# Summing a state-space scan over its states by accumulating transposes instead of identity matmuls

## The chip, the cores and the metric

The kernel runs on one core of one Trainium2 chip. A core has five engines that work side by side, each through its own list of instructions in order: TensorE (PE, with its weight loads shown as PEld), VectorE (DVE), ScalarE (ACT), GpSimd (POOL) and SyncE (SP, which here issues the transfers). They wait for one another through semaphores. The metric is the device time of one execution in microseconds (us), the median of three runs.

## The reference

The reference chains four layers over 8 images of 192 channels and 64 x 64 positions. Layers 0 and 2 each hold a selective state-space scan in four directions (rows, columns, and both reversed), and these two scans per image are what the change is about. For each direction, per channel c and state n (16 states):

```python
xs = jnp.stack([x_hw, x_wh, x_hw[..., ::-1], x_wh[..., ::-1]], axis=1)
x_dbl = jnp.einsum('kdc,bkcl->bkdl', x_proj_w, xs)
dts, Bs, Cs = (x_dbl[:, :, :R], x_dbl[:, :, R:R + N], x_dbl[:, :, R + N:])
dt = jax.nn.softplus(jnp.einsum('kcr,bkrl->bkcl', dt_proj_w, dts) + dt_proj_b[None, :, :, None])
A = -jnp.exp(A_log)
...
def step(h, inp):
    dt_t, B_t, C_t, x_t = inp
    h = h * jnp.exp(dt_t[..., None] * A[None]) + (dt_t * x_t)[..., None] * B_t[:, :, None, :]
    return (h, jnp.einsum('bkcn,bkn->bkc', h, C_t))
_, ys = jax.lax.scan(step, h0, (dt_l, Bs_l, Cs_l, xs_l))
ys = jnp.moveaxis(ys, 0, 3) + Dp[None, :, :, None] * xs
```

So the state h is a first-order recurrence along 4096 positions, and the output at a position is the sum over the 16 states of h times C. The four directions are added up at the end. All numbers are float32.

## The kernel before, in words

The kernel runs the images one after the other. For each there are two calls of `scan_layer`, and between them the rest of the layers, which the change leaves alone. There are 16 scans in all.

**Units.** Channels are on the 128 partitions; the four scan directions with 192 channels fill three such blocks, v = 0, 1, 2 (v = 2 holds the 64 remaining channels of two directions), and a forward pass (d = 0) and a backward pass (d = 1). A pass goes over the positions in 8 chunks of Q = 512. One unit is (d, chunk, v): 2 x 8 x 3 = 48 units in a scan. A group m is the three units of one chunk. Within a unit the 512 positions are four blocks of 128 (NB = 4, SB = 128), and the tile `da` is laid out as 128 x [4 blocks, 16 states, 128 positions].

**A unit's work.** It is done in eight steps j = 0..7; two steps make one block, one for each half of the states.
- `fill` (L288, PE) makes the driving term u for a step in PSUM, by 16 or 32 small matmuls of 32 rows. Tile `u` has two buffers.
- `scan` (L304, L306, L309, DVE) runs the recurrence over 8 states x 128 positions in place in `da`.
- `times_c` (L326, POOL) multiplies a finished block by C, which `load_c` (L263, L266) has brought in as a broadcast of 1 MB; then L329 (POOL) adds the top three or four states' planes onto lower ones, so that 12 or 13 planes of 16 are left to sum (NP = 12).
- `add_up` (L344, L349, PE) adds the planes over the states: matmuls of the identity with 512 positions of one state, accumulating in the PSUM tile `py`. The table SUM says how many come in each step. The sums of unit k-1 run during unit k, from step 2 on.
- `finish` (L372 or L376, DVE) takes the sum out of PSUM two units later, at step 2. In the forward pass it adds the skip term and stores the result to the DRAM tensor `yp`; in the backward pass it adds what `load_y` has fetched of `yp` and stores to `ys`.

**Preparation of the next unit.** `steps_a` (PE, L212 or L214), `steps_b` (ACT softplus, L218) and `steps_c` (POOL, L222) make the time steps and their product with the input. `turn` transposes that product at step 2 on PE (L230) and ACT copies it out (L232, then four pieces L235). `decay` (L245, ACT) makes the 16 exponentials of the next unit's `da` at steps 2 to 6, and `cut` (L254, L255) and `keep` (L316) hand over the ends of blocks and chunks at step 7. For the next group, `project_a` and `project_b` (L147, L154, L157) stand at steps 0 and 1 of v = 0, `diagonals_a` (L187) at step 5 of v = 1 and step 1 of v = 2, and `diagonals_b` (DVE, L197) at steps 6 and 7 of both.

**What sets the order.** The whole scan stands under a hand-written order: each engine works through its instructions as the loop over k and j lists them, and waits where data or a buffer are missing. In one step the loop lists scan, (step 7) cut and keep, times_c and load_c, steps_c, fill of the next step, finish, load_y, turn, projections and diagonals, add_up, decay.

**PSUM** is full: `da0` one bank, `u` four, `misc` two, `py` one. `misc` is shared by turn, the projections, steps_a and diagonals_a. At step 4 of v = 0, two `misc` buffers are taken by steps_a for the next group; they are read by the softplus at step 1 of v = 1. `da` has three buffers, `ct` three.

Of the kernel before, what the change touches and what calls it, by code (L numbers as in the profile page):

```python
# [40 lines left out]
def tile_net(ctx: ExitStack, tc: tile.TileContext, a: dict, out: bass.AP):  # L41
# [23 lines left out]
    yp = [dram.tile([P, T], F32, name=f"yp{i}") for i in range(3)]  # L65
# [33 lines left out]
    def scan_layer():  # L99
# [5 lines left out]
        with (  # L105
# [11 lines left out]


            NP = 12
# [6 lines left out]
            dts, dtx, dtt, das, cts, us, py, yo = {}, {}, {}, {}, {}, {}, {}, {}  # L126
# [5 lines left out]
            def misc():  # L132
                return sp.tile([P, Q], F32, tag="misc", name="misc", bufs=2)
# [86 lines left out]
            def steps_c(k):  # L220
                dtx[k] = sw.tile([P, Q], F32, tag="dtx", name="dtx")
                nc.gpsimd.tensor_tensor(dtx[k], dts[k], vt[k // 3][:, units[k][3], :], ALU.mult)  # L222
# [95 lines left out]
            def times_c(k, g):  # L318
                h = das[k][:, NB - 1 - g if units[k][0] else g]
                if k == nu - 1 and g == NB - 1:  # L320

                    ct = cts.pop((k, g))
                    for eng, n in ((nc.gpsimd, slice(0, 8)), (nc.vector, slice(8, NS))):
                        eng.tensor_tensor(h[:, n], h[:, n], ct[:, n], ALU.mult)
                    return
                nc.gpsimd.tensor_tensor(h, h, cts.pop((k, g)), ALU.mult)  # L326
                n = NS - NP if g < 2 else NS - NP - 1
                to = h[:, NP - n : NP]
                nc.gpsimd.tensor_tensor(to, to, h[:, NS - n : NS], ALU.add)  # L329

            def load_y(k):
                d, i, c, v = units[k]
                yo[k] = sw.tile([P, Q], F32, tag="yo", name="yo")
                if d:
                    nc.sync.dma_start(out=yo[k], in_=yp[v][:, c * Q : (c + 1) * Q])

            to_add = []

            def add_up(count):

                for k, n in to_add[:count]:
                    if n == 0:
                        py[k] = sp.tile([P, Q], F32, tag="py", name="py")
                    nc.tensor.matmul(  # L344
                        py[k], ident, das[k][:, :, n, :], start=(n == 0), stop=(n == NP - 1)
                    )
                    if n == 8:
                        s = slice(0, NB // 2) if units[k][0] else slice(NB // 2, NB)
                        nc.tensor.matmul(  # L349
                            py[k][:, s.start * SB : s.stop * SB], ident, das[k][:, s, NP, :],  # L350
                            start=False, stop=False,
                        )
                del to_add[:count]

            def add_last(g0, g1):

                k = nu - 1
                if k not in py:
                    py[k] = misc()
                s = slice(NB - g1, NB - g0)  # L360
                ns = NS if g1 == NB else NP + (g0 == 2)
                for n in range(ns):
                    nc.tensor.matmul(  # L363
                        py[k][:, s.start * SB : s.stop * SB], ident, das[k][:, s, n, :],
                        start=(n == 0), stop=(n == ns - 1),
                    )

            def finish(k):
                d, i, c, v = units[k]
                p, y = py.pop(k), yo.pop(k)  # L370
                if d == 0:
                    nc.vector.scalar_tensor_tensor(  # L372
                        y, vt[k // 3][:, v, :], skip[:, v : v + 1], p, ALU.mult, ALU.add
                    )
                else:
                    nc.vector.tensor_tensor(y, y, p, ALU.add)  # L376
                nc.sync.dma_start(out=(ys if d else yp)[v][:, c * Q : (c + 1) * Q], in_=y)

            SUM = ((1, 0, 1, 2, 0, 2, 1, 2), (2, 2, 1, 1, 1, 2, 2, 2), (2, 1, 1, 2, 2, 2, 2, 2))
            DECAY = {2: (0, 3), 3: (3, 7), 4: (7, 9), 5: (9, 12), 6: (12, 16)}

            def has(k):
                return 0 <= k < nu
# [27 lines left out]
            for k in range(nu + 1):  # L413
                m, v = divmod(k, 3)
                ahead = 0 <= m + 1 < nm
                for j in range(8):
# [20 lines left out]
                    if j == 2:  # L437
                        if has(k - 2):
                            finish(k - 2)
                        if k == nu:  # L440
                            finish(k - 1)
                        if has(k - 1) and k < nu:
                            load_y(k - 1)
                        if has(k + 1):
                            turn(k + 1)
# [20 lines left out]
                    if (k, j) == (nu - 1, 3):  # L466
                        load_y(k)
                    if j == 2 and has(k - 1) and k < nu:
                        to_add += [(k - 1, n) for n in range(NP)]
                    add_up(SUM[v][j])  # L470
                    if (k, j) == (nu - 1, 7):
                        add_last(0, 2)
                    if (k, j) == (nu, 0):
                        add_up(NP)
                        add_last(2, 3)
                        add_last(3, 4)
# [880 lines left out]
```

## Time and profile before

| | |
|---|---|
| median of three runs | 25583.9 us (25560.59 to 25592.02) |
| span of the profiled execution | 25584.6 us |
| one scan, first to last recurrence (16 of them, the 4th as example) | 1154.9 us |
| DMA over the span | 4294 MB, mean 168 GB/s |
| ACT copy of 128 x 512 out of PSUM (L232), mean | 587 ns |
| exponentials (L245), mean of one | 699 ns, 12544 of them |
| PE matmuls of the sums (L344), mean of one | 627 ns, 18048 of them |
| PE matmuls of the turn (L230), mean of one | 317 ns, 3072 of them |

The profile page gives, for each engine, the time in which it was busy and its share of the span. PE's time is that of overlapping matmuls, so its share says how long something was in flight and not how near PE is to its limit; the start of one group and the start of the next say more. The groups list for each line of the kernel the number of instructions, the busy time, the mean of one, and the idle time before it with what ended it. The chain of waits is followed back from the last instruction. In answers by stretch of time, each engine has its busy time with the number of instructions in brackets, then come the granted TensorE clock as a share of full speed, the share of the DMA engines, and GB/s. In a timeline, a line is start, duration, engine, line, operation, tiles and the number of instructions merged.

### The profile page before, as it was taken

Reading aid. Unit: us, or ns where it says so; the run is one execution under the profiler, and the core shown is the slowest. Engines: PE = TensorE matmul, PEld = TensorE weight load, DVE = VectorE, ACT = ScalarE, POOL = GpSimd, SP = SyncE. Lnnn points to the kernel's source line nnn. Section 1 sums busy time; section 2 is a strip of 40 time slices with the busy share of each in tenths; the row PEclk is TensorE's granted clock in tenths of the full one; section 3 lists DMA queues with packets and bytes.
Section 4 is the critical chain, followed back from the end, with each engine's and each line's share of the span. In section 5 each row is a group of like instructions: output and inputs, shape, how many; then the busy total and the mean of one; then the engine's idle time right before and its main releaser. Section 6 shows DMA issues by size and latency. Waiting matters only on the chain.

```text
span 25584.6 us, 433060 instructions
## 1 busy us (share of the span) xinstructions
PE 23083.5 (90%) x174856; PEld 12129.3 (47%) x174856; DVE 20590.3 (80%) x21253; ACT 14175.8 (55%) x23120; POOL 19097.7 (75%) x7436
## 2 busy tenths in 40 slices
PE   9989889898898988989889898898988989899896
PEld 4535445353453534535345353553535535355353
DVE  7969789697896968969689696886968879688795
ACT  5646456464564645646456564555645556455563
POOL 7939589395893958939589395894958949589495
PEclk9989989899998999989999899998999989899898
DMA  5636556365563655636556365663655636566364
GB/s 168 207 116 203 145 173 207 117 202 146 174 206 115 204 146 171 206 117 204 141 177 204 120 202 138 180 202 119 204 134 182 202 120 204 131 185 204 118 204 117
DMA packets 1204805, 4293.98 MB, mean 168 GB/s; under 512 B 360224, under 2 KB 419456, under 8 KB 804480
## 3 DMA queue, kind: packets, MB, share of 16 engines
q1 hardware_dynamic: 1202816, 4266.25, 56.3%
q8 instruction: 1395, 22.86, 0.4%
q14 instruction: 594, 4.87, 0.1%
HBM read 3810.55 MB, written 450.72 MB: 167 GB/s over the span
## 4 chain that ended last, share of the span: by engine, by line
POOL 36%; PE 13%; DVE 5%; ACT 4%; issue 3%; DMA 2%; SPq 0%; POOLq 0%; DVEq 0%; ACTq 0%
POOL da L326 27%; POOL da L329 6%; PE py L344 3%; PE u L288 2%; POOL dtx L222 2%; DVE da L309 2%; PE pa L530 1%; ACT da L245 1%; PE pa L533 1%; DMA a<-t 1%; PE misc L363 1%; DVE pwc L986 0%; DMA t<-u 0%; PE paa L530 0%; PE pac L530 0%
## 5 line engine op out<-in xcount | busy, mean ns | idle before, releaser
L309 DVE TENSOR_TENSOR_SCAN da<-da,u 128x1024 f32<-128x1024 f32 x6144 | 14042.1, 2286 | 325.4 <-ACT da L255 37.0
L326 POOL TENSOR_TENSOR da<-da,ct 128x2048 f32<-128x2048 f32 x3056 | 13859.0, 4535 | 319.9 <-DVE tmp L304 297.3
L344 PE MATMUL py<-da,ident 128*128 128x512 f32 x18048 | 9304.0, 627 | 504.0 <-POOL da L326 407.0
L288 PEld LDWEIGHTS u<-dg,dtt 32*128 32x128 f32 x131072 | 5943.9, 163 | 4598.2 <-issue 4309.6
L245 ACT ACTIVATE da<-dt,neg_a 128x512 f32<-128x512 f32 (+1 forms) x12544 | 7662.1, 699 | 16.3
L288 PE MATMUL u<-dg,dtt 32*128 32x128 f32 x131072 | 7234.0, 283 | 120.7 <-DVE da L309 48.2
L344 PEld LDWEIGHTS py<-da,ident 128*128 128x128 f32 x18048 | 3043.1, 191 | 2998.5 <-issue 2134.8
L329 POOL TENSOR_TENSOR da<-da 128x512 f32<-128x512 f32 (+1 forms) x3056 | 3474.4, 1137 | 239.6
L222 POOL TENSOR_TENSOR dtx<-dt,vt 128x512 f32<-128x512 f32 x768 | 979.1, 1276 | 3310.1 <-ACT dt L218 2621.4
L232 ACT COPY dtt<-misc 128x512 f32<-128x512 f32 x768 | 450.4, 587 | 3343.3 <-PE misc L230 3343.3
L306 DVE TENSOR_TENSOR u<-u,tmp 128x8 f32<-128x8 f32 x5952 | 1009.9, 170 | 1081.2 <-PE u L288 860.0
L235 ACT COPY dtt<-misc 32x512 f32<-32x512 f32 x3008 | 1734.7, 577 | 45.3
L197 DVE TENSOR_TENSOR dg<-msk,misc 128x1024 f32<-128x1024 f32 x1024 | 1222.9, 1197 | 439.1 <-DMA vt<-vs 239.3
L161 ACT ACTIVATE xd<-misc,msk 128x512 f32<-128x512 f32 x256 | 175.7, 686 | 1790.7 <-PE misc L157 1790.7
L218 ACT ACTIVATE dt<-misc 128x512 f32<-128x512 f32 x768 | 430.8, 595 | 1101.7 <-PE misc L214 1096.7
L974 POOL TENSOR_TENSOR acc<-u,gate 128x486 f32<-128x486 f32 (+1 forms) x80 | 108.5, 1360 | 962.0 <-DVE u L989 688.8
L930 POOL MEMSET t<- 128x4356 f32 (+2 forms) x32 | 100.5, 3140 | 932.7 <-DVE t L904 914.6
L968 PE MATMUL pwc<-t,l3taps 128*128 128x486 f32 (+1 forms) x1280 | 590.7, 610 | 40.2 <-DVE t L989 20.1
L230 PE MATMUL misc<-ident,dtx 128*128 128x128 f32 x3072 | 592.7, 317 | 0.0
L187 PE MATMUL misc<-ident,xd 16*128 16x16 f32 x4096 | 565.5, 266 | 26.0 <-DVE dg L197 26.0
L986 DVE SCALAR_TENSOR_TENSOR pwc<-t,l3p,pwc 128x486 f32<-128x486 f32 (+1 forms) x640 | 467.0, 736 | 136.6 <-PE pwc L968 123.8
L187 PEld LDWEIGHTS misc<-ident,xd 16*128 16x128 f32 x4096 | 528.2, 210 | 92.7 <-issue 88.9
(291 smaller groups left out, 18289.2 us busy)
## 6 DMA issues: line engine op xcount, KB each, us to landing
ct<-cd SPq DMA_DIRECT2D x2048, 1024.0 KB
ct<-cd SPq DMA_DIRECT2D x2048, 512.0 KB
vt<-vs SPq DMA_DIRECT2D x768, 256.0 KB
yp<-yo SPq DMA_DIRECT2D x384, 256.0 KB
yo<-yp SPq DMA_DIRECT2D x384, 256.0 KB
ys<-yo SPq DMA_DIRECT2D x384, 256.0 KB
yt<-ys SPq DMA_DIRECT2D x96, 512.0 KB
t<-ys SPq DMA_DIRECT2D x96, 512.0 KB
```

The lines of the kernel that those rows point to most:

```text
L187: nc.tensor.transpose(pt[:, i * NS : (i + 1) * NS], xd[m][rows, cols], ident[rows, rows])
L197: nc.vector.tensor_tensor(dg[m, o][:, at], msk[:, 0:32].unsqueeze(1).unsqueeze(1).to_broadcast(shape), bts[m, o][:, at, r * 8 : r * 8 + 8] ...
L222: nc.gpsimd.tensor_tensor(dtx[k], dts[k], vt[k // 3][:, units[k][3], :], ALU.mult)
L230: nc.tensor.transpose(pt[:, i * P : (i + 1) * P], dtx[k][:, cols], ident)
L235: (nc.scalar.copy if k else nc.vector.tensor_copy)(dtt[k][q * 32 : (q + 1) * 32, 1], pt[r * 32 : (r + 1) * 32])
L245: nc.scalar.activation(das[k][:, s, n, :], dts[k].rearrange("p (s t) -> p s t", t=SB)[:, s], AF.Exp, scale=neg_a[:, v, d, n : n + 1],)
L288: nc.tensor.matmul(u[ch, r * 4 : r * 4 + 4, e::4], dtt[k][rows, r, e, ch], dg[k // 3, o][rows, r * 4 + e, n], start=True, stop=True,)
L306: nc.vector.tensor_tensor(head, head, tmps[k][:, n], ALU.add)
L309: nc.vector.tensor_tensor_scan(h, h, u.rearrange("p n t -> p (n t)")[:, way], 0.0, ALU.mult, ALU.add)
L326: nc.gpsimd.tensor_tensor(h, h, cts.pop((k, g)), ALU.mult)
L329: nc.gpsimd.tensor_tensor(to, to, h[:, NS - n : NS], ALU.add)
L344: nc.tensor.matmul(py[k], ident, das[k][:, :, n, :], start=(n == 0), stop=(n == NP - 1))
```

## The change

- `times_c` no longer adds planes together: L327 to L329 go.
- `add_up` no longer multiplies by the identity with the data as the moving operand. It takes one plane of 128 positions of one state as the stationary operand, in transpose mode, with the identity moving, and accumulates the 16 states of a block in PSUM. The result `py` is turned: positions on the partitions, channels along the free dimension. There are 16 transposes for a block, eight in a step, and a block's transposes begin two steps after its product with C is listed. So a unit's sums run from its own step 4 to step 3 of the next.
- `take` is new: at step 4 of the next unit ACT copies `py` to the tile `yt`. In the forward pass that is stored at once to `yp`, which now is positions by channels in DRAM.
- `load_y` fetches `yp` in that form at step 2, in the backward pass only, into one buffer instead of two.
- `turn_back` is new, backward pass only: at step 6 eight transposes on PE turn this pass's sums and the stored ones back and add them, in a `misc` buffer.
- `finish` now is in the backward pass only, at step 7: it adds the skip term and stores to `ys`.
- `dtx` has one buffer instead of two. The table SUM, the constant NP and the special end `add_last` go.

```diff
-                n = NS - NP if g < 2 else NS - NP - 1
-                to = h[:, NP - n : NP]
-                nc.gpsimd.tensor_tensor(to, to, h[:, NS - n : NS], ALU.add)
+            def positions(v, c):
+                return yp[v][c * Q : (c + 1) * Q].rearrange("(s t) c -> t s c", s=NB)
...
                 if d:
-                    nc.sync.dma_start(out=yo[k], in_=yp[v][:, c * Q : (c + 1) * Q])
+                    yo[k] = sw.tile([P, NB, P], F32, tag="yo", name="yo", bufs=1)
+                    nc.sync.dma_start(out=yo[k], in_=positions(v, c))
...
+            def add_up(block, part):
+                k, g = divmod(block, 4)
+                if g == 0 and part == 0:
+                    py[k] = sp.tile([P, NB, P], F32, tag="py", name="py")
+                s = NB - 1 - g if units[k][0] else g
+                for n in range(part * 8, part * 8 + 8):
                     nc.tensor.matmul(
-                        py[k], ident, das[k][:, :, n, :], start=(n == 0), stop=(n == NP - 1)
+                        py[k][:, s], das[k][:, s, n, :], ident, is_transpose=True,
+                        start=(n == 0), stop=(n == NS - 1),
                     )
...
+            def take(k):
+                d, i, c, v = units[k]
+                yt[k] = sw.tile([P, NB, P], F32, tag="yt", name="yt")
+                nc.scalar.copy(yt[k], py.pop(k))
+                if d == 0:
+                    nc.sync.dma_start(out=positions(v, c), in_=yt.pop(k))
+            def turn_back(k):
+                pb[k] = misc()
+                new, old = yt.pop(k), yo.pop(k)
+                for s in range(NB):
+                    for x in (new, old):
                         nc.tensor.matmul(
+                            pb[k][:, s * P : (s + 1) * P], x[:, s], ident, is_transpose=True,
+                            start=(x is new), stop=(x is old),
                         )
...
             def finish(k):
+                y = sw.tile([P, Q], F32, tag="y", name="y", bufs=1)
+                nc.vector.scalar_tensor_tensor(
+                    y, vt[k // 3][:, v, :], skip[:, v : v + 1], pb.pop(k), ALU.mult, ALU.add
+                )
+                nc.sync.dma_start(out=ys[v][:, c * Q : (c + 1) * Q], in_=y)
...
-                    add_up(SUM[v][j])
...
+                    if has(k - 1) and j == 4:
+                        take(k - 1)
+                    block = (8 * k + j - 4) // 2
+                    if 0 <= block < 4 * nu:
+                        add_up(block, j % 2)
+                    if has(k - 1) and units[k - 1][0]:
+                        if j == 6:
+                            turn_back(k - 1)
+                        if j == 7:
+                            finish(k - 1)
                     if has(k + 1) and j in DECAY:
                         decay(k + 1, *DECAY[j])
```

More of the change, by code (lines that the diff above doesn't have):

```diff
@@ L64, in tile_net @@
     ys = [dram.tile([P, T], F32, name=f"ys{i}") for i in range(3)]
-    yp = [dram.tile([P, T], F32, name=f"yp{i}") for i in range(3)]
+    yp = [dram.tile([T, P], F32, name=f"yp{i}") for i in range(3)]
     a_scr = dram.tile([192, T], F32, name="a_scr")
@@ L116, in scan_layer @@
             nck = T // Q
-            NP = 12
             units = [
@@ L125, in scan_layer @@
             vt, xd, cdr, dg = {}, {}, {}, {}
-            dts, dtx, dtt, das, cts, us, py, yo = {}, {}, {}, {}, {}, {}, {}, {}
+            dts, dtx, dtt, das, cts, us = {}, {}, {}, {}, {}, {}
+            py, yo, yt, pb = {}, {}, {}, {}
             def chunk_of(m):
@@ L220, in steps_c @@
             def steps_c(k):
-                dtx[k] = sw.tile([P, Q], F32, tag="dtx", name="dtx")
+                dtx[k] = sw.tile([P, Q], F32, tag="dtx", name="dtx", bufs=1)
                 nc.gpsimd.tensor_tensor(dtx[k], dts[k], vt[k // 3][:, units[k][3], :], ALU.mult)
@@ L326, in times_c @@
                 nc.gpsimd.tensor_tensor(h, h, cts.pop((k, g)), ALU.mult)
-                n = NS - NP if g < 2 else NS - NP - 1
-                to = h[:, NP - n : NP]
-                nc.gpsimd.tensor_tensor(to, to, h[:, NS - n : NS], ALU.add)
+            def positions(v, c):
+                return yp[v][c * Q : (c + 1) * Q].rearrange("(s t) c -> t s c", s=NB)
             def load_y(k):
                 d, i, c, v = units[k]
-                yo[k] = sw.tile([P, Q], F32, tag="yo", name="yo")
@@ L334, in load_y @@
                 if d:
-                    nc.sync.dma_start(out=yo[k], in_=yp[v][:, c * Q : (c + 1) * Q])
[L337 to L343, printed above, removed]
+                    yo[k] = sw.tile([P, NB, P], F32, tag="yo", name="yo", bufs=1)
[6 more added lines that the diff above has]
+                for n in range(part * 8, part * 8 + 8):
@@ L344, in add_up @@
                     nc.tensor.matmul(
-                        py[k], ident, das[k][:, :, n, :], start=(n == 0), stop=(n == NP - 1)
-                    )
-                    if n == 8:
-                        s = slice(0, NB // 2) if units[k][0] else slice(NB // 2, NB)
+                        py[k][:, s], das[k][:, s, n, :], ident, is_transpose=True,
+                        start=(n == 0), stop=(n == NS - 1),
+                    )
+            def take(k):
[4 more added lines that the diff above has]
+                    nc.sync.dma_start(out=positions(v, c), in_=yt.pop(k))
@@ L349, in add_up @@
+            def turn_back(k):
[3 more added lines that the diff above has]
+                    for x in (new, old):
                         nc.tensor.matmul(
-                            py[k][:, s.start * SB : s.stop * SB], ident, das[k][:, s, NP, :],
-                            start=False, stop=False,
-                        )
[L353 to L366, printed above, removed]
+                            pb[k][:, s * P : (s + 1) * P], x[:, s], ident, is_transpose=True,
+                            start=(x is new), stop=(x is old),
+                        )
@@ L368, in finish @@
             def finish(k):
                 d, i, c, v = units[k]
[L370 to L381, printed above, removed]
+                y = sw.tile([P, Q], F32, tag="y", name="y", bufs=1)
@@ L437, in scan_layer @@
                     if j == 2:
[L438 to L442, printed above, removed]
+                        if has(k - 1):
                             load_y(k - 1)
@@ L465, in scan_layer @@
                             diagonals_b(m + 1, v - 1, j - 6)
[L466 to L469, printed above, removed]
-                    add_up(SUM[v][j])
[L471 to L476, printed above, removed]
+                    if has(k - 1) and j == 4:
[8 more added lines that the diff above has]
+                            finish(k - 1)
                     if has(k + 1) and j in DECAY:
```

## The prediction

> **What bounds the kernel now.** I read the page first: busy shares, chain, groups.
>
> ```profile
> PE 23083.5 (90%) x174856; PEld 12129.3 (47%) x174856; DVE 20590.3 (80%) x21253; ACT 14175.8 (55%) x23120; POOL 19097.7 (75%) x7436
> ...
> POOL da L326 27%; POOL da L329 6%; PE py L344 3%; PE u L288 2%; POOL dtx L222 2%; DVE da L309 2%; PE pa L530 1%; ACT da L245 1%; PE pa L533 1%; DMA a<-t 1%; PE misc L363 1%; DVE pwc L986 0%; DMA t<-u 0%; PE paa L530 0%; PE pac L530 0%
> ...
> L309 DVE TENSOR_TENSOR_SCAN da<-da,u 128x1024 f32<-128x1024 f32 x6144 | 14042.1, 2286 | 325.4 <-ACT da L255 37.0
> L326 POOL TENSOR_TENSOR da<-da,ct 128x2048 f32<-128x2048 f32 x3056 | 13859.0, 4535 | 319.9 <-DVE tmp L304 297.3
> ...
> L329 POOL TENSOR_TENSOR da<-da 128x512 f32<-128x512 f32 (+1 forms) x3056 | 3474.4, 1137 | 239.6
> L222 POOL TENSOR_TENSOR dtx<-dt,vt 128x512 f32<-128x512 f32 x768 | 979.1, 1276 | 3310.1 <-ACT dt L218 2621.4
> ```
>
> PE looks fullest by share, but the chain of waits runs on POOL. So I took the scans alone, then stretches of one, busy times with the granted clock (the figure before the DMA share):
>
> ```profile
> 4901.20:6056.10 1154.90, 1117.06 (x9985) 644.11 (x9984) 1055.81 (x1050) 724.23 (x1249) 1131.70 (x428) 0.98 0.65 200
> ...
> 1712.30:1735.30 23.00, 20.08 (x126) 14.01 (x124) 19.45 (x17) 21.12 (x44) 15.93 (x6) 0.50 0.28 94
> 1735.30:1767.10 31.80, 31.51 (x173) 18.98 (x174) 22.07 (x21) 18.07 (x30) 27.89 (x12) 0.52 0.60 191
> 1767.10:1791.80 24.70, 24.70 (x286) 14.07 (x286) 22.35 (x20) 13.62 (x24) 21.80 (x9) 1.00 0.52 139
> ...
> 2799.90:2803.30 3.40, 2.66 (x28) 1.59 (x24) 3.37 (x3) 0.00 (x0) 3.32 (x3) 1.00 0.18 58
> 2803.30:2806.70 3.40, 1.84 (x20) 1.56 (x20) 3.23 (x5) 1.25 (x3) 3.40 (x1) 1.00 0.61 251
> 2806.70:2810.10 3.40, 3.04 (x12) 1.54 (x14) 2.64 (x4) 3.34 (x6) 3.32 (x3) 0.50 0.51 214
> ```
>
> One scan is 1154.9 us for 48 units; POOL is busy 98% of it. The first unit takes 23 us, so a steady unit takes 1132/47 = **24.1 us**. POOL's work per unit is 4 x 4.535 (L326) + 4 x 1.137 (L329) + 1.276 (L222) = 24.0: POOL sets the pace now. The second thing to see is the clock. One stretch of 3.4 us with PE busy only 1.84 us is followed by a clock of 0.50. The first unit, with fills and no sums yet, stays at 0.50. The next unit, at 0.52, takes 31.8 us where its successor at 1.00 takes 24.7. POOL is far from full there: PE paces it, 31.51 of 31.8 us.
>
> **POOL and DVE after the change.** POOL loses L329: 19.4 us a unit. DVE's floor comes from starts of L309 where nothing is late: an odd step follows an even one after 2.39 us (5020.40, 5022.79), an even one after 2.81 (5028.65, 5031.46), and the next unit after 2.76. So 4 x 2.39 + 3 x 2.81 + 2.76 = 20.75; L197 in two units of three adds two times 1.13 each, mean 1.5, in all 22.25. The finish (0.72) leaves DVE in the first direction and stays in the second: 22.25 and 22.97, mean **22.6**. That is what the change could reach: 1.5 us less in each of 47 x 16 = 752 units.
>
> **PE.** Removed are 25 half-sums' worth of streaming: 24 instructions of L344 and 2 of L349. Two instructions take about 1.05 us with their switch, so some 12 us a unit. Added are 64 transposes, eight in a step. No row shows transposes that accumulate. The nearest are L230 (four, 0.59 us from the first to the next line's start) and L187 (eight, 1.06). If they go as these do, eight take 1.0 us, 8.0 a unit; if each is two passes, as L344's sums are, 2.0 and 16. I take 1.0: L230 has the same size and mode. With eight fills of 1.09, one turn, L187 and the projections, PE has about 20 us a unit at full clock, so in total it would fit below DVE. At clock 0.50 it does not:
>
> ```profile
> 4930.60 2.08 PE L288 MATMUL u<-dg,dtt 32*128 32x128 f32 x16
> 4932.60 1.13 PE L230 MATMUL misc<-ident,dtx 128*128 128x128 f32 x4
> 4933.53 1.91 PE L344 MATMUL py<-da,ident 128*128 128x512 f32 x2
> ```
>
> A fill takes 2.0 us (start to start), four transposes 0.93, so eight 1.8. A step is 3.8 us of PE.
>
> **The new wait.** Tile py has one buffer. The first transpose of unit k (step 4) must wait until take has read unit k-1's sums, and take stands on ACT at step 4 behind the whole turn and seven decays. All this starts from the turn on PE at step 2:
>
> ```profile
> 5051.12 0.75 PE L230 MATMUL misc<-ident,dtx 128*128 128x128 f32 x4
> ...
> 5051.91 0.59 ACT L232 COPY dtt<-misc 128x512 f32<-128x512 f32 x1 [0.71 <-PE misc L230]
> 5052.50 2.34 ACT L235 COPY dtt<-misc 32x512 f32<-32x512 f32 x4
> ...
> 5054.87 7.46 ACT L245 ACTIVATE da<-dt,neg_a 128x512 f32<-128x512 f32 x12
> ```
>
> From turn to first decay 3.75 us, seven decays at 7.46/12 = 0.62 are 4.35, take itself is a copy like L232, 0.59: **8.7 us**. In units with v = 1 a table load stands before the decays (1.28): 10.0. Meanwhile PE, at full clock, needs from the turn 0.55 + 1.0 + 1.1 + 1.0 + 1.1, waiting a little for scans: it has finished the fill for step 5 some 5 to 5.5 us after the turn. It then stands for 3.2 to 3.7 us (4.5 to 5 for v = 1). Queued behind the waiting transpose is the fill for step 6, and DVE's scan 6 waits for that. After the wait come 1.0 (eight transposes) and 1.4 (fill start to scan start): scan 6 starts 11.1 us after the turn, where it now starts 5060.92 - 5051.12 = 9.8 after. That is 1.3 us lost per unit even at full clock, on the engine that would pace it.
>
> **What the wait does to the clock.** PE standing for over 3 us in each unit leaves a stretch of 3.4 us with at most 1.8 us of work, like the row that lost the clock. I conclude that each unit drops to 0.50 at step 4. When does it return? From the rows, full-height matmuls raise it and 32-row fills do not: in the scan from 4901.2 the clock comes back in the second unit (0.75 over 4924.2 to 4949.5), whose first sums stand at 4933.53 above. Alternating fills and transposes look just short of it; a projection, or two groups of eight transposes running on, looks enough.
>
> Here a rule speaks against the change: the Trainium skill, "TensorE: Matmul & The Clock Gate", Part 4: PE-mode transpose, says that transposes do not count as PE work for the clock in the way that matmuls do. No row here has transposes in bulk. By that rule the clock would never come back, and the sum would be the ceiling below, 34.6 ms.
>
> **The sum.** Take to next turn is six fills and six groups of transposes; at 0.50, 6 x 3.8 = 22.8; turn to take 8.7; base 31.5. *First direction*: v = 0 has the projections L147 and L154/L157 (+2.0 and +1.0), which bring the clock back and make the last three items short (-2.6): 31.9. v = 1 has L214 at 2.0, a table load 1.3, and gains 0.9: 33.9. v = 2 has eight L187 at half clock, 1.8: 33.3. Mean 33.0. *Second direction*: turn_back's eight transposes follow eight others at step 6; after 4 x 1.8 + 2 x 2.0 = 11.2 us the clock returns and DVE paces: + 1.4 + 2.39 + 2.29 to the end of scan 1, + 1.8 to 2.0 to the turn, + 8.7 or 10.0: 28.0, 29.1, 27.9. Another wait belongs to it: at v = 0, step 6, turn_back wants a misc buffer, but both hold the projections of step 4 until the softplus at step 1 of the next unit, which ACT reaches only after keep, that is after scan 7. I price it at 3 us once in three units. Mean 29.3. Over both 31.15, against 24.1: +7.1 x 752 = +5,300 us. The profiled span is 25,584.6, the median of the runs 25,583.9, so no correction: **30,900 us**. Check from a row: the unit at clock 0.52 took 31.8.
>
> **Costed at nothing.** take adds 0.59 to ACT, busy 724 of 1155 us. Stores and loads of yp go in runs of 512 B instead of 2 KB; number and bytes are unchanged. load_y stands on SP behind the ct load that waits for POOL's product, and its data are needed at step 6 instead of a unit later. At 28 us a unit some 14 us cover it; at 22.6 it could be late by 0 to 2 us. dtx with one buffer: its reader, the turn, is three steps earlier. The end of each scan changes by sixteen transposes, a copy and eight more against add_last: -5 to +5 us, 16 times.
>
> **Rivals.** *Clock holds* (1.00 as now, if such gaps don't drop it): the units are DVE's floor plus 1.3 for take, 1.28 for v = 1, about 0.7 for fills late behind projections, and 1.4 in the second direction for the misc wait (4.3/3): 24.75 and 26.85, mean 25.8: 25,584 + 1.75 x 752 = 26,900. For it: the clock is 0.98 in scans today. Against: the 1.84 row. *Faster*: DVE at its floor, 25,584 - 1.45 x 752 = 24,500. It needs take done within 7.4 us of the turn instead of 8.7, in every unit, and no misc wait. For it: POOL's 4.5 us really go. Against: the ACT lines above are in this order today. *Clock never returns*: eight steps of 3.8, turn 0.9, L187 1.2, projections 2.6, turn_back 0.9: 36.0; +11.9 x 752: 34,600. *It doesn't do what it says*: transposes in two passes, full clock: 8 x 1.0 more PE, some 28 us a unit, 28,500; that lies inside the forecast's side.
>
> **Numbers.** Clock falls at the take wait (28,500 to 34,600): 0.62. Clock holds, waits cost: 0.21. DVE floor: 0.14. No change (within 0.2%, about what a measurement here can tell): 0.03. So faster 0.14, same 0.03, slower 0.83. The range leaves out the faster cases: 26,000 to 34,600; the forecast's own is 28,500 to 34,600.
>
> **What would show it.** POOL's share of the chain falls and ACT's and PE's rise; the first transposes of a unit wait for ACT take; the granted clock in the scans is well below 0.98 (about 0.6 to 0.7 here); POOL idles. Wrong if the scans keep a clock near 1.00 (then 26.9 ms), or if scan 6 is not late behind take (then 24.5).

## The result and the profile after

| | before | after |
|---|---|---|
| median of four runs, us | 25,576.62 (25,560.59 to 25,592.02) | 31,722.15 (31,661.19 to 31,799.55) |
| ratio, 95% interval | | 1.2406, 1.2386 to 1.2426: slower |
| span of the profiled execution, us | 25,584.6 | 31,714.0 |
| one scan, mean of 16, us | 1156.0 | 1546.5 |
| all that is not scans (span less 16 scans), us | 7,089 | 6,970 |
| mean granted clock over the span | 0.938 | 0.708 |

The whole loss is in the scans: 16 x 390.5 = 6,248 us, less the 119 us by which the rest got shorter.

From the page of the kernel after: busy times, the granted clock in 40 slices, the chain of waits (by engine, by line), and three groups.

```profile
PE 26927.9 (85%) x206216; PEld 19752.3 (62%) x206216; DVE 20433.0 (64%) x20869; ACT 14567.1 (46%) x23888; POOL 15710.4 (50%) x4380
...
PEclk6676766767667676676766768677686676867767
...
issue 10%; POOL 8%; PE 5%; DVE 1%; ACT 1%; DMA 1%; SPq 0%; POOLq 0%; ACTq 0%; DVEq 0%
POOL da L324 7%; PE u L286 1%; PE py L343 1%; POOL dtx L220 0%; PE pa L517 0%; ACT da L243 0%; DVE da L307 0%; PE pa L520 0%; DVE pwc L973 0%; DMA a<-t 0%; ACT dtt L233 0%; DMA t<-u 0%; PE pac L517 0%; POOL t L1008 0%; POOL acc L961 0%
...
L324 POOL TENSOR_TENSOR da<-da,ct 128x2048 f32<-128x2048 f32 x3056 | 13848.9, 4532 | 10129.2 <-DVE tmp L302 5493.5
L343 PE MATMUL py<-ident,da 128*128 128x128 f32 x49152 | 9794.0, 365 | 2550.7 <-ACT yt L351 1832.7
L286 PE MATMUL u<-dg,dtt 32*128 32x128 f32 x131072 | 10126.2, 364 | 92.5 <-DVE da L307 50.9
L304 DVE TENSOR_TENSOR u<-u,tmp 128x8 f32<-128x8 f32 x5952 | 1016.3, 171 | 7041.7 <-PE u L286 6932.8
```

The change did what it says: L329 is gone and POOL's busy time with it (19,098 to 15,710 us). Yet POOL now stands 10,129 us ahead of its products, where it stood 320. Follow who waits for whom: POOL waits for DVE, and DVE waits 6,933 us for PE's fills (L304 ended by L286). PE waits 1,833 us for ACT's take (L343 ended by L351). The profile puts some waits of the same place down to POOL (dtx); but in 736 of 752 units a unit's first transpose starts within 0.15 us of the end of take, and the time that PE stands idle there (a stand, from here on) adds up to 2,542 us. That is still too little to explain 6,000. The clock row points to the rest: 6s and 7s, a mean of 0.708 where the kernel before had 0.938. The chain of waits itself names little, since most of its shares are spread over lines below one per cent.

A timeline of one unit with v = 1 shows the wait (columns: start, duration, engine, line, operation, tiles, number merged, and in brackets the idle time before with what ended it):

```profile
4962.94 0.75 PE L228 MATMUL misc<-ident,dtx 128*128 128x128 f32 x4
4963.53 1.04 PE L343 MATMUL py<-ident,da 128*128 128x128 f32 x8
4963.73 0.59 ACT L230 COPY dtt<-misc 128x512 f32<-128x512 f32 x1 [2.62 <-PE misc L228]
4964.33 2.34 ACT L233 COPY dtt<-misc 32x512 f32<-32x512 f32 x4
...
4966.61 1.16 PE L286 MATMUL u<-dg,dtt 32*128 32x128 f32 x16
4966.68 1.28 ACT L243 ACT_TABLE_LOAD   x1
4967.97 4.40 ACT L243 ACTIVATE da<-dt,neg_a 128x512 f32<-128x512 f32 x7
...
4972.27 0.57 ACT L351 COPY yt<-py 128x512 f32<-128x512 f32 x1
...
4972.98 1.94 PE L343 MATMUL py<-ident,da 128*128 128x128 f32 x8 [5.21 <-ACT yt L351]
...
4974.85 2.08 PE L286 MATMUL u<-dg,dtt 32*128 32x128 f32 x16
4976.98 0.17 DVE L304 TENSOR_TENSOR u<-u,tmp 128x8 f32<-128x8 f32 x1 [6.01 <-PE u L286]
```

PE turns at 4962.94 and has finished its fill by 4967.77. The next transposes stand until take has emptied `py`: 5.21 us. The fill behind them is late, and DVE stands 6.01. Read the durations on both sides of the stand as well: eight transposes took 1.04 us ahead of it and 1.94 behind it, sixteen small matmuls 1.16 and 2.08. The same stretch in windows of 3.4 us (columns: stretch, its length, busy time and number of instructions of PE, PEld, DVE, ACT, POOL, then granted clock, DMA share, GB/s), and below it one whole scan:

```profile
4964.30:4967.70 3.40, 3.40 (x43) 2.82 (x41) 3.23 (x4) 3.35 (x6) 1.85 (x1) 1.00 1.01 343
4967.70:4971.10 3.40, 0.07 (x2) 0.00 (x0) 3.20 (x4) 3.39 (x7) 3.40 (x2) 1.00 0.34 131
4971.10:4974.50 3.40, 1.52 (x7) 1.55 (x8) 0.00 (x0) 3.40 (x7) 3.40 (x2) 0.61 0.76 198
4974.50:4977.90 3.40, 3.40 (x27) 3.03 (x27) 0.89 (x2) 3.40 (x7) 1.58 (x1) 0.50 0.72 152
6059.50:7601.30 1541.80, 1366.43 (x11995) 1129.89 (x11994) 1047.03 (x1025) 746.54 (x1293) 920.95 (x238) 0.67 0.49 150
```

Full clock before the stand, half behind it. This is so throughout. Leaving out the first group and the last of each scan, there are 112 units of each kind (a v in a direction) in the 16 scans. In all 112 the clock drops once during step 5, in the stand or up to 1.4 us behind the end of take. The one exception is v = 2 of the first direction (28 of 112), which mostly is at 0.50 before it gets there.

### The profile page after: what moved, and what is told of

Same layout as the page of the kernel before. It is cut to its first block, busy times and chain, and to the rows that moved or that the text cites. A ratio compares the mean times of both kernels' runs of the same rounds, so it can differ in the third digit from the quotient of the medians.

```text
span 31714.0 us, 493761 instructions
## 1 busy us (share of the span) xinstructions
PE 26927.9 (85%) x206216; PEld 19752.3 (62%) x206216; DVE 20433.0 (64%) x20869; ACT 14567.1 (46%) x23888; POOL 15710.4 (50%) x4380
## 5 line engine op out<-in xcount | busy, mean ns | idle before, releaser
L343 PE MATMUL py<-ident,da 128*128 128x128 f32 x49152 | 9794.0, 365 | 2550.7 <-ACT yt L351 1832.7
L343 PEld LDWEIGHTS py<-ident,da 128*128 128x128 f32 x49152 | 7979.3, 190 | 4293.9 <-issue 2579.8
L286 PE MATMUL u<-dg,dtt 32*128 32x128 f32 x131072 | 10126.2, 364 | 92.5 <-DVE da L307 50.9
L286 PEld LDWEIGHTS u<-dg,dtt 32*128 32x128 f32 x131072 | 8447.9, 222 | 1764.5 <-issue 1632.4
L243 ACT ACTIVATE da<-dt,neg_a 128x512 f32<-128x512 f32 (+1 forms) x12544 | 7740.7, 701 | 12.8
L304 DVE TENSOR_TENSOR u<-u,tmp 128x8 f32<-128x8 f32 x5952 | 1016.3, 171 | 7041.7 <-PE u L286 6932.8
L314 ACT COPY carry<-da 128x16 f32<-128x16 f32 x672 | 146.1, 217 | 2814.9 <-DVE da L307 2814.9
L361 PE MATMUL misc<-ident,yt 128*128 128x128 f32 x1536 | 628.2, 412 | 285.2 <-ACT dt L216 274.3
L351 ACT COPY yt<-py 128x512 f32<-128x512 f32 x768 | 432.9, 564 | 493.4 <-PE py L343 493.4
L145 PE MATMUL misc<-vt,wxt 128*128 128x512 f32 x512 | 433.2, 941 | 253.3 <-DMA vt<-vs 244.5
L361 PE MATMUL misc<-ident,yo 128*128 128x128 f32 x1536 | 621.1, 408 | 10.3 <-DMA yo<-yp 10.2
L185 PEld LDWEIGHTS misc<-ident,xd 16*128 16x128 f32 x4096 | 541.7, 212 | 115.8 <-issue 114.3
```

What stands on the lines that cost most here:

```text
L243: nc.scalar.activation(das[k][:, s, n, :], dts[k].rearrange("p (s t) -> p s t", t=SB)[:, s], AF.Exp, scale=neg_a[:, v, d, n : n + 1],)
L286: nc.tensor.matmul(u[ch, r * 4 : r * 4 + 4, e::4], dtt[k][rows, r, e, ch], dg[k // 3, o][rows, r * 4 + e, n], start=True, stop=True,)
L304: nc.vector.tensor_tensor(head, head, tmps[k][:, n], ALU.add)
L343: nc.tensor.matmul(py[k][:, s], das[k][:, s, n, :], ident, is_transpose=True, start=(n == 0), stop=(n == NS - 1),)
L361: nc.tensor.matmul(pb[k][:, s * P : (s + 1) * P], x[:, s], ident, is_transpose=True, start=(x is new), stop=(x is old),)
```

## The experiments

The theory: PE stands behind take; the stand takes the clock; at half clock PE paces the unit. The rival: the stands themselves (take, and turn_back's wait for a `misc` buffer) make the loss, and the low clock only goes with it. Ratios are to the kernel before, run on the same chip, with their 95% intervals.

**e1: no wait for take.** `py` gets a second buffer. PSUM is full, so `da0` goes to SBUF to make room for it, and `yt` has one buffer.

```diff
-            da0 = sp.tile([P, 2, NB, NS], F32, name="da0")
+            da0 = sw.tile([P, 2, NB, NS], F32, name="da0", bufs=1)
-                    py[k] = sp.tile([P, NB, P], F32, tag="py", name="py")
+                    py[k] = sp.tile([P, NB, P], F32, tag="py", name="py", bufs=2)
-                yt[k] = sw.tile([P, NB, P], F32, tag="yt", name="yt")
+                yt[k] = sw.tile([P, NB, P], F32, tag="yt", name="yt", bufs=1)
```

> Edit: py gets a second buffer; for its PSUM bank, da0 moves to SBUF, and yt goes from two buffers to one to make room. Nothing else moves. Theory A (PE stands behind take, that drops the clock, and the low clock makes the loss): the first direction's units lose the gap before their first transpose, the granted clock there is above 0.9 and a unit takes 23 to 24.5 us; in the second direction the misc wait at step 6 of v = 0 remains and still costs a stand and a dip of the clock, units 25 to 29 us. In all 26,000 to 27,500 us. Theory B (transposes do not hold the clock whatever stands between them): the clock in the scans stays below 0.75 and the time at 30,000 us or more. Theory C (PE has simply too much work): as B in time, but PE without gaps at a clock near 1.

29,116.16 us, 1.1389 (1.1356 to 1.1423): better than after by 2,600 us, but 1,600 above what was expected. Of the drops of the clock (from full to half) none is left at step 5; of the 736 in the scans, 424 are at step 7 now, 200 at step 1 and 93 at step 0. The timeline of e1 shows a cost that the theory did not have, at the start of a unit:

```profile
5813.92 4.52 POOL L324 TENSOR_TENSOR da<-da,ct 128x2048 f32<-128x2048 f32 x1 [1.99 <-ACT carry L314]
...
5814.62 3.84 DVE L302 TENSOR_TENSOR tmp<-da,carry 128x16 f32<-128x16 f32 x1
```

A product of 128 x 16 numbers takes 3.84 us and ends when POOL's product does. The making of room is itself expensive, so this run confounds two things. e9 measures the second.

**e9: the kernel before, with `da0` in SBUF alone** (the first pair of lines of the diff above).

> Edit on the kernel before: da0 alone moves from PSUM to SBUF, to read by itself what came with the second py buffer, where one DVE product of 128 x 16 (tmp, both inputs in SBUF) was seen at 3.84 us beside a POOL product of 4.52. If DVE with two SBUF inputs has to wait for POOL's running product, tmp's 0.18 us grows to some 2 us on the mean (half of 4.5), four times in a unit, and the kernel before gets slower by 1,000 to 4,000 us, as POOL is busy nearly always there. If the 3.84 us came from something else, the time stays within 1% and tmp near 0.2 us.

28,823.37 us, 1.1277 (1.1255 to 1.13), within what was expected. The kernel before, then e9, by the source line of the product (instructions, least/median/most ns, first and last start, shape):

```profile
L304 DVE TENSOR_TENSOR tmp<-da,da x2304: 175/177/184, 188.2 to 25156.8; 128x16 f32<-128x16 f32 x192
L304 DVE TENSOR_TENSOR tmp<-da,carry x672: 147/166/176, 252.8 to 25140.3; 128x16 f32<-128x16 f32 x168
```

```profile
L304 DVE TENSOR_TENSOR tmp<-da,da x2304: 184/188/1916, 187.2 to 28390.4; 128x16 f32<-128x16 f32 x192
L304 DVE TENSOR_TENSOR tmp<-da,carry x672: 150/3843/4431, 255.6 to 28372.8; 128x16 f32<-128x16 f32 x168
```

I had expected all four products of a unit to be held; only the first was (166 to 3,843 ns). Setting the starts beside POOL's products explains it: in e9, 2,272 of the 2,304 later products (tmp<-da,da) started while no product of POOL was running, and the 32 that did overlap one had a median of 1,410 ns. In the kernel before, 2,163 of them started while one ran, with `da0` in PSUM, and took 177. So in these runs a DVE product with both inputs in SBUF waits for POOL's running one; with one input in PSUM it doesn't. The price is 3,265 us for the kernel, 4.3 us a unit (over 752). The clock falls with it, from 0.937 to 0.865 over the span, and its share in the price was not taken apart. e1, e3 and e4 carry this cost, and none can be set against after for the price of the stand.

**e2: take earlier.** take moves from step 4, behind seven decays, to step 3, behind three of them.

```diff
-                    if has(k - 1) and j == 4:
-                        take(k - 1)
...
+                    if has(k - 1) and j == 3:
+                        take(k - 1)
```

> Edit: take moves from step 4 to the end of step 3, ahead of four of the seven decays it stood behind. py keeps one buffer. Theory A: take ends some 6.2 us after the turn instead of 8.6 (7.5 with v = 1's table load), and PE stands only about 1 us (2.3 us for v = 1), so the clock mostly holds in v = 0 and v = 2 of the first direction and the time is 26,500 to 29,000 us. Theory B: clock below 0.75, 30,000 us or more. If the length of the stand did not matter (any wait drops the clock), it would stay near 31,000.

28,172.13 us, 1.102 (1.0965 to 1.1075): 3,550 us less than after. Drops at step 5 are gone at v = 0. For v = 1, where the table load still stands before take, they stay (112 and 109 of 112). In the second direction 96 more are at step 7 of v = 0, where turn_back waits for its buffer.

**e5: the other wait.** steps_a, which holds both `misc` buffers from step 4 of v = 0 to the softplus of the next unit, moves to step 0 of v = 1, just ahead of that softplus.

```diff
-                    if ahead and (v, j) == (0, 4):
+                    if ahead and (v, j) == (1, 0):
+                        steps_a(k + 2)
...
-                        steps_a(k + 4)
```

> Edit on the changed kernel: the two steps_a matmuls that hold both misc buffers from step 4 of v = 0 move to step 0 of v = 1, so that turn_back at step 6 finds a buffer. The take wait stays. Theory A with the misc wait as a separate cost: DVE's step 7 to 0 at v = 0 of the second direction, now about 8.8 us against 2.8, loses some 5 us; once in three units of the second direction, that is 112 times 5 to 9 us with what the clock does: 30,700 to 31,200 us. If the misc wait is hidden by the take wait: no change, 31,700.

30,802.24 us, 1.205 (1.2015 to 1.2085): as expected, 920 us less than after. It is the second direction that gains: there a steady group of three units (medians) takes 29.4 + 31.4 + 28.0 = 88.8 us, against 33.5 + 37.7 + 27.8 = 99.0 in the kernel after. In the first direction the mean unit is 33.1 in both.

**e6: the stand filled with work that nobody reads.** e5, and in front of the waiting transposes four matmuls into a spare `misc` buffer. The stand's end is still set by take, which ends 8.60 us behind the turn at v = 0 and 9.89 at v = 1, as in after (8.62 and 9.89); PE only isn't idle in it, but for the last 0.29 us at v = 0 and 1.58 at v = 1.

```diff
+                    if has(k - 1) and has(k) and j == 4:
+                        junk = misc()
+                        for _ in range(4):
+                            nc.tensor.matmul(
+                                junk, ident, wxt.rearrange("p d j m -> p (d j m)"), start=True, stop=True
+                            )
```

> Edit: as the kernel with steps_a moved, and four 128 x 512 matmuls of the identity and a constant into a free misc buffer ahead of the transposes that wait for take; da0 stays in PSUM this time. The output is untouched. To be read against the kernel with steps_a moved alone. Theory A: the clock no longer drops, over 0.9 in the scans; the direct price of the wait stays (some 3.4 us of DVE per unit), units near 26.5 us, 27,000 to 28,500 us. Rival (the stand is the loss, the clock a by-product): within 2% of the kernel with steps_a moved alone, in spite of the higher clock.

27,873.67 us, 1.0904 (1.083 to 1.0978). Against e5 that is 2,929 us, 9.5%, for adding work. One scan of e5, then one of e6, in the columns of the windows above:

```profile
5884.00:7378.20 1494.20, 1312.53 (x11992) 1088.25 (x11991) 1045.92 (x1025) 746.61 (x1293) 920.54 (x238) 0.70 0.50 154
```

```profile
5319.20:6608.10 1288.90, 1203.73 (x12371) 921.57 (x12370) 1036.24 (x1025) 746.67 (x1293) 923.37 (x238) 0.91 0.59 179
```

PE does some 380 more instructions in the scan (188 matmuls, two each), is in flight for 109 us less, and has a clock of 0.91 instead of 0.70 (0.89 and 0.70 on the mean of the 16 scans); DVE, ACT and POOL do the same work. The rival is out as the main cause: take stands where it stood, and more than half of e5's loss (2,929 of 5,242 us) is gone. At v = 0 of the first direction, where the clock is 1.00 in all steps, the unit takes 22.97 us. Of the 308 drops left in the scans, 123 are at step 1 of v = 2, where the sixteen-row transposes of diagonals_a (L185) run, 86 at step 1 of v = 0 in the second direction, and 69 at step 5 of v = 1, whose stand the filling doesn't cover to its end.

**e3 and e4: matmuls or transposes as the filling.** after, with `da0` in SBUF (and its cost) to free a bank for the filling: four matmuls of 128 x 512 in e3, 28 transposes of 128 x 128 in e4.

```diff
+                    if has(k - 1) and has(k) and j == 4:
+                        for _ in range(4):
+                            nc.tensor.matmul(junk, ident, wide, start=True, stop=True)
```

```diff
+                        for i in range(28):
+                            nc.tensor.matmul(
+                                junk[:, i % 4 * P : (i % 4 + 1) * P], ident, ident,
+                                is_transpose=True, start=True, stop=True,
+                            )
```

> Edit: the take wait stays as it is; before the transposes that stand behind it, PE gets four 128 x 512 matmuls of the identity and a constant into a bank that nobody reads (da0 in SBUF and yt with one buffer, as in the kernel with two py buffers). The output is untouched. At full clock they take 4 x 0.85 = 3.4 us and lie in the stand. Theory A: the wait's direct price stays, but the clock no longer drops in the first direction: above 0.9 there, units of 24 to 26 us, and 26,500 to 29,000 us in all, so more work on PE makes the kernel faster. Rival (the stand itself is the loss and the clock a by-product): no faster than 31,000 us. Theory B: slower than 31,700, since it adds work.

> Edit: as the kernel with four matmuls in the stand, with 28 transposes of the identity (28 x 0.12 = 3.4 us) in their place. The output is untouched. If transposes count for the clock like matmuls of the same height, the result is that of the four matmuls within 3%. If they don't count, the clock drops in each unit as in the changed kernel and the time is 31,000 us or more.

30,742.6 us, 1.2026 (1.1991 to 1.2061), and 30,463.54 us, 1.1917 (1.1882 to 1.1951). e3 is outside of what was expected, with the cost of `da0` that e9 shows in it. e4 is what was expected if transposes count: 0.9% from e3. Span and mean clock of e3 and then of e4:

```profile
core 0: 30740.4 us, clock 0.832
```

```profile
core 0: 30449.2 us, clock 0.832
```

These are means over the whole kernel. The stand itself is seen in step 5 of v = 0. Three such steps follow, in after, e3 and e4, in the columns of the windows above:

```profile
6360.10:6366.60 6.50, 3.62 (x28) 2.90 (x27) 2.66 (x4) 6.50 (x12) 6.50 (x3) 0.84 0.41 169
```

```profile
6149.00:6155.20 6.20, 6.20 (x37) 3.66 (x36) 3.32 (x3) 6.20 (x12) 6.08 (x3) 1.00 0.40 168
```

```profile
6115.50:6121.20 5.70, 5.70 (x57) 5.17 (x56) 3.32 (x3) 5.70 (x11) 5.57 (x3) 1.00 0.52 144
```

At v = 0, where either filling covers the stand, the clock drops at step 5 in none of the 240 units of e3 and in none of e4, against all 240 in after. So transposes hold the clock there as matmuls do. At v = 1 of the first direction a stand is left behind the filling, 1.58 us in e3 and 2.01 in e4, and the clock drops in 2 and in 62 of 128 units.

**e7: both waits eased** (the edits of e2 and e5 together).

> Edit: take at the end of step 3, and steps_a moved to step 0 of v = 1. Theory A: both waits are short, except in v = 1, where the table load keeps the stand at over 2 us; the clock falls there and comes back at the next projection. v = 0 near 22.5 us, v = 1 near 26, v = 2 near 28 in the first direction; 26,500 to 27,500 us. If the clock were lost for another reason than stands, it would stay below 0.8.

28,491.59 us, 1.1146 (1.1093 to 1.1199): a miss, and no better than e2 alone (1.102). The second direction gained (29.8 to 26.6 us a unit, mean of the six inner groups), the first lost (27.0 to 29.3). In e2, steps_a at step 4 of v = 0 happened to fill the stand; with it moved, the clock drops at step 5 of v = 0 in the first direction too (63 of 112 units; none in e2). It is e6 the other way round: taking work out of the stand costs. The same first transposes of such a unit, in e2, in e7 and in after (where the profile names POOL, and take ended 0.14 us earlier), show how long PE stood:

```profile
5687.60 1.06 PE L343 MATMUL py<-ident,da 128*128 128x128 f32 x8 [0.42 <-ACT yt L351]
```

```profile
5761.90 1.06 PE L343 MATMUL py<-ident,da 128*128 128x128 f32 x8 [1.47 <-ACT yt L351]
```

```profile
6363.34 1.06 PE L343 MATMUL py<-ident,da 128*128 128x128 f32 x8 [2.88 <-POOL dtx L220]
```

Each is within 0.02 us in all 112 units of its run. So 0.42 us cost the clock in none, 1.47 in 63, and 2.88 in all.

**e8: the table load out of take's way.** e7, and a one-column exponential right behind the softplus, so that the table is loaded before the turn.

```diff
+                        nc.scalar.activation(warm, eps, AF.Exp)
```

> Edit: as the kernel with take early and steps_a moved, and an exponential of one column on ACT right after the softplus of step 1 in v = 1, so that the table load happens while ACT waits for the turn. Theory A: the last stand of over 2 us goes; the clock holds above 0.95 through the scans, units near DVE's floor plus PE's lateness behind projections, 23 to 24.5 us: 24,700 to 26,000 us. If it does not hold, transposes and fills alone are below what the clock asks in some stretches, and the time stays above 26,500.

26,533.84 us, 1.038 (1.0285 to 1.0476): 500 above the range, but 1,958 us less than e7 for moving a load of 1.28 us. The edit moves 240 of them, so that is 8.2 us for each. The load's own 1.28 is the smaller part; that the rest comes through the clock, which rises from 0.757 to 0.824 over the span, is likely but was not measured apart. Of the 496 drops in the scans, 283 are still at step 5, 91 at step 0, and 109 at steps 1 and 7 of v = 2 in the first direction.

**e10, e11, e12: every remaining gap held.** e8, with diagonals_a of v = 2 at step 5, and unread matmuls where PE is thin: in e10 one at step 4, and one each at steps 6 and 7 of v = 1 and 2 behind a unit of the first direction. e11 has two at step 4. e12 is e10 with one more at steps 0 and 1 of v = 2 in the second direction, where 79 of e10's last 95 drops were.

```diff
-                        if j == (5, 1)[v - 1]:
+                        if j == 5:
...
+                    busy = 0
+                    if has(k - 1) and has(k):
+                        if j == 4:
+                            busy = 1
+                        elif j >= 6 and v > 0 and not units[k - 1][0]:
+                            busy = 1
+                        elif j < 2 and v == 2 and units[k - 1][0]:
+                            busy = 1
```

> Edit: take early, steps_a moved, table load early (as in the kernel with those three); further diagonals_a of v = 2 moves from step 1 to step 5, and one 128 x 512 matmul that nobody reads goes ahead of the transposes at step 4, and one each at steps 6 and 7 of v = 1, 2 in units whose predecessor is in the first direction. The output is untouched. Theory A: the drops at step 5 and around the diagonals become rare, clock above 0.95 in the scans, units of 22.5 (v = 0) to 24.5 us; 24,700 to 25,700 us, so at or below the kernel before. If the clock still falls in more than one unit of four: 25,900 to 26,600 us.

> Edit: as the kernel with one filling matmul at step 4, with two there. Theory A: fewer drops still, and PE some 0.85 us later behind step 4, which DVE's scan 6 feels by at most that: 24,600 to 25,900 us. If the clock already holds with one, this is slower by 0 to 2%.

> Edit: as the kernel with one filling matmul at step 4, with one more at each of steps 0 and 1 of v = 2 in units whose predecessor is in the second direction, the one place where that kernel still lost the clock (79 times in its 16 scans). The output is untouched. Theory A: no drops in the scans, v = 2 of the second direction from 26.0 to about 23.7 us, 112 times 2.3 us less: 24,550 us, which is DVE's floor as the prediction worked it out (24,500). If the work on PE is now the limit there, 24,800 or more.

| | median, us | ratio to before, 95% | mean unit of the six inner groups, first and second direction, us |
|---|---|---|---|
| e10 | 24,809.35 | 0.9706 (0.9692 to 0.9721) | 22.62, 23.89 |
| e11 | 24,864.38 | 0.9724 (0.9708 to 0.974) | 22.78, 23.89 |
| e12 | 24,574.15 | 0.9606 (0.9593 to 0.9619) | 22.62, 23.06 |

The second matmul of e11 gains nothing: its four runs all lie above e10's four, by 55 us at the median. e12 beats both kernels. One scan of it, in the columns of the windows:

```profile
4712.50:5816.40 1103.90, 1050.94 (x12181) 825.49 (x12180) 1035.37 (x1025) 747.88 (x1308) 922.79 (x238) 0.98 0.70 209
```

and its chain of waits:

```profile
DVE 12%; PE 6%; ACT 4%; issue 2%; DMA 1%; POOL 1%; SPq 0%; DVEq 0%; POOLq 0%; ACTq 0%
DVE da L308 9%; ACT da L244 2%; PE u L287 1%; DVE dg L196 1%; PE py L344 1%; PE pa L532 1%; DVE u L305 1%; ACT dtt L234 1%; POOL da L325 0%; DVE tmp L303 0%; PE pa L535 0%; DVE pwc L988 0%; DMA a<-t 0%; DMA t<-u 0%; PE pac L532 0%
```

The clock is 0.98 again, DVE is busy 1035 of 1104 us, and its recurrence (L308) leads the chain. Up to step 6 of a unit the recurrences start every 2.39 and 2.81 us in turn, with nothing late in between.

From after to e12 the way is: e5 for the `misc` wait, -920; e6 for the clock in the stand, -2,929; e10 for take's place, the table load, one matmul in the stand instead of four and the gaps of v = 1 and 2, together -3,064 and not taken apart further; e12 for the last two steps, -235. (Differences of medians from several chips; the kernel before, run on each, agreed within 0.12%.)

A second `py` buffer with `da0` left in PSUM wasn't tried: no bank is free for it.

## Why the prediction held, and which terms were off

The time lay inside the range, 2.7% above the forecast of 30,900 us, and the mechanism was the one forecast: the wait for take, and the clock that goes with it.

**POOL stops pacing; DVE's floor is 22.25 and 22.97.** Held. POOL idles in after, and e12, where the clock holds, runs at 22.62 and 23.06. Most of the 0.37 in the first direction is at the end of v = 0, where the next unit's first recurrence starts after 3.70 us instead of 2.76. In e12 DVE's first product there waits for ACT's cut, which comes right behind the exponentials:

```profile
4879.43 0.18 DVE L303 TENSOR_TENSOR tmp<-da,carry 128x16 f32<-128x16 f32 x1 [0.83 <-ACT da L253]
```

That e12's 24,574 us stand so near the 24,500 of the "faster" case is partly luck: the rest of the kernel, outside of the scans, came out 141 us shorter than before.

**Eight transposes 1.0 us, 1.8 at half clock; a fill 2.0.** Held: 1.04, 1.94 and 2.08, and some 0.07 less from start to start. So the two-pass case is out.

**From turn to take 8.7 us, 10.0 with the table load.** Held: medians of 8.6 to 9.0, and of 9.9 and 10.3 for v = 1 in the two directions. **PE stands 3.2 to 3.7, and 4.5 to 5 for v = 1.** Roughly held: medians of 5.21 and 4.22 for v = 1, but 2.88 for v = 0, where the matmuls of steps_a at step 4 stand in front of the transposes. The working left them out; with them moved away (e5) it is 3.93. At v = 2 of the first direction, at half clock, PE stands 0.57.

**The stand takes the clock in every unit.** Held but for v = 2 of the first direction, which mostly hadn't got it back; and e6 shows that the clock, not the stand, carries most of the loss. The first direction's units came out at 32.1, 34.3 and 33.05 us, against 31.9, 33.9 and 33.3. Where the clock comes back was in part a guess, for no row had groups of transposes. It was borne out at v = 0 of the first direction (step 1 or 2, with the projections) and at v = 1 and 2 of the second (step 7, behind turn_back, in 240 units). One reading in the working was too strong: in the unit at 0.52 POOL was not far from full, with 27.89 of 31.8 us; that PE paced it rests on PE's 31.51.

**The wait for `misc`, 3 us once in three units.** This is the term that was mis-sized. A timeline of step 7 of v = 0 in the second direction, after:

```profile
7157.67 1.28 ACT L216 ACT_TABLE_LOAD   x1
7158.97 1.09 ACT L216 ACTIVATE dt<-misc 128x512 f32<-128x512 f32 x2
...
7159.62 0.47 PE L361 MATMUL misc<-ident,yt 128*128 128x128 f32 x1 [2.86 <-ACT dt L216]
```

The stand itself, 2.86 us until the softplus has read its buffer, is near the price of 3 us. But with what the low clock behind it costs, the wait makes the group 10.2 us longer than in e5 (99.0 against 88.8). Of this 4.1 are in v = 0, and 6.3 in v = 1, whose recurrences still start 3.81 and 3.91 us apart at clock 0.50: the prediction let turn_back's transposes bring the clock back in every unit of the second direction, and behind a stand of 3 us they don't: at v = 0 it comes back at step 7 only in the last group, where no steps_a holds the buffers, and otherwise at step 2 or 3 of v = 1. It had asked where the clock returns behind take, and not behind this second stand. A group was put at 88.0 and took 99.0; over six steady groups of 16 scans this 11.0 is 1,056 us. The median missed by 822; the rest of the kernel, for one, came out 119 us shorter.

**The price of the stand at full clock, 1.3 us.** Mis-sized too, with no weight in the sum, which went by half clock, but in the "clock holds" case. In e6, at clock 1.00 (v = 0), step 5 takes 5.00 us where the floor is 2.81: 2.2. The working compared scan 6 with its place in the kernel before, where it was already late: there scans 2 to 6 take 11.38 us at v = 0, and at DVE's floor 10.40. The difference is the finish, which stands between two recurrences on DVE, and a fill that comes late:

```profile
5051.80 0.72 DVE L372 SCALAR_TENSOR_TENSOR yo<-vt,skip,py 128x512 f32<-128x512 f32 x1
...
5057.90 0.17 DVE L306 TENSOR_TENSOR u<-u,tmp 128x8 f32<-128x8 f32 x1 [0.16 <-PE u L288]
```

The 1.3 was then added to a floor without them, so about 1.0 was left out, and the case's 26,900 was too cheap by that. By the same working the "faster" case needed take done some 6.5 us behind the turn, not 7.4; in e12 it is 6.16 in every kind of unit.

**The rule against transposes.** The Trainium skill, "TensorE: Matmul & The Clock Gate", Part 4: PE-mode transpose, has it that transposes don't engage the clock. The runs differ, and the measurement decides: with the stand of v = 0 filled, step 5 is at 1.00 with transposes (e4) as with matmuls (e3), and e12, whose sums are all transposes (with 95 unread matmuls in a scan), keeps 0.98. The ceiling of 34,600 (its sum gives 34,530) that went by the clock never returning was not reached; in after the clock comes back ahead of every stand but most of those at v = 2 of the first direction, or it could not drop again in each.

## What to carry to other kernels

Price a new wait on TensorE twice: for the time that it stands, and for what the work behind it costs at half clock, and ask again at every later wait whether the clock has come back. Where a stand can't be removed at once, work that nobody reads can pay for itself (-9.5% here), and work that looks misplaced may be what holds the clock. A price taken against a kernel in which the same place was already late must not be added to the floor of the new one.

## What the runs showed of the hardware

- One stretch of 3.4 us with 0.07 us of PE work, followed by one with 1.52, took the clock from 1.00 to 0.50. At v = 0 of the first direction a stand of 0.42 us took it in 0 of 112 units, one of 1.47 in 63 and one of 2.88 in all. With take at step 3 and the table loaded early, one unread matmul of 128 x 512 at each thin step (e12) keeps it at 0.98 over the scans; two at step 4 (e11) are no better than one (e10).
- Transposes of 128 x 128 held the clock in the stand as matmuls of 128 x 512 did: 1.00 in step 5 of v = 0 in e4 and e3, 0.84 in the same step of after.
- DVE and POOL get in each other's way by where the inputs lie: 0.166 us against 3.843 for the same 128 x 16 product, when its PSUM input moves to SBUF while POOL multiplies. The Trainium skill, "GPSIMD Engine Reference", section 1. Specifications, names the interfaces that the two share and DVE instructions with two SBUF inputs as a case of contention; the runs agree, and in e9 the kernel is 13% longer for it, the lower clock that comes with it included.
